# A two-layer graph-attention kernel: one attention block per turn, and a new order of the turn

## The chip, the cores and the metric

The kernel runs on one core of a Trainium2 chip. The metric is device time in microseconds (us) of one execution; a median of several runs is given, and one further execution was recorded by the hardware profiler. TensorE is called PE below, VectorE DVE, ScalarE ACT, GpSimd POOL, SyncE SP (its DMA queue SPq).

## What is computed

Input x is 128 graphs of 128 nodes with 512 features, adj a mask per graph. Two layers follow each other. Layer 0 is masked attention with 4 heads of 64, layer 1 layer-normalises its input once more, has 8 heads of 64 and lets each node see itself. All is float32.

```python
# layer 0
q, k, v = (split_heads(x @ W) for W in (Wq, Wk, Wv))
sim  = where(adj, q @ k.T * 64 ** -0.5, -max)
x    = layernorm(x + (softmax(sim) @ v) @ Wo + bo)
# layer 1
h    = layernorm(x) * gamma + beta
q, k, v = split(h @ w_qkv.T)
sim  = where(adj | eye, q @ k.T * 64 ** -0.5, -1e9)
out  = layernorm(x + (softmax(sim) @ v) @ w_out.T + b_out)
```

## The kernel before, in words

**Tiling.** Two graphs (b = 0, 1) make a group g; there are NG = 64 groups. R[g] holds a group's rows (128 nodes on the partitions, 2 x 512 features) from loading to storing. Every large matrix product (qkv of layer 0, qk and v of layer 1, and the output projections of both) is done as seven smaller block products in place of eight (1, 2, ..., 7 in the code, a Strassen-like scheme): sums of blocks of the activations are made by POOL (`sums`, `out_sums`, L281 to L291), sums of blocks of the weights once at the start by DVE (`weight_sums`). The products accumulate in three PSUM banks, "a", "f" and "c". `INTO` (L296) tells which product goes where, and which one starts its bank: 1, 6, 7, 4 go into a one after the other, 5 and 3 into f, 2 into c. After 1, 5 and 6 the running value is copied out by ACT (`eqk1`, `eqk5`, `eqk6` for layer 1's q and k, `ev` for v, `e` for layer 0), and the DVE later adds such a copy to what 2, 7 and 3 left. So product 7 cannot write bank a before ACT has read it for `eqk6`, and product 3 cannot write f before ACT has read it for `eqk5`.

**The pipeline over groups.** The kernel is an opening, a loop of turns `step(s)` for s = 2 to 63, and four turns `closing(s)`. All order is written out by hand (manual schedule): each engine carries its instructions out in the order in which the program issues them. A turn works on several groups at once: layer 0's qkv of group s (`product_0`), scores and softmax of layer 0 for group s - 1 and of layer 1 for group s - 3, attention and output projection of layer 0 for group s - 2 and of layer 1 for group s - 4, v and the last qk product of group s - 3, and qk of group s - 2.

**Attention before.** The turn has two half-turns, k = 2s and 2s + 1, one for each graph of a group. `scores(k)` (L435) computes the scores of both layers for one graph into four PSUM tiles; `cleared` (POOL) fills the softmax tiles with the mask value, `masked` (DVE, L466) copies the scores where the mask is set and takes the maxima, `exps` (ACT, L490) takes exponentials with their sums, `normalised` (L499, POOL) multiplies by the reciprocal sums. The transposition of the probabilities is done in three steps: `blocks` (L502) transposes 32 x 32 blocks on DVE, a DMA puts the result into DRAM (`put`, L204), and four DMAs fetch it with the blocks in place (`fetch`, L210, by `probs_arrive`). `attend(s)` (L543) multiplies the probabilities of both graphs and both layers by v, once per turn.

**Activations are transposed in the same way.** `turn(l, g)` (L219) transposes blocks of R[g] on DVE and puts them into DRAM (`scr`), `arrive` fetches four pieces (`raw`). For layer 0, `in_order(g)` (L246) copies raw to xT on ACT and calls `sums`; for layer 1, `finish(g, half)` (L259) does it with gamma and beta. `turn(0, s+1)` and `in_order(s+1)` bring the next group's xT for the next turn. In turns 2 and 3 (`direct`) layer 1's input is transposed on PE (`finish_direct`).

**Other steps.** `addend(l, g)` (L581, POOL) adds the bias to R[g]; for layer 1 ACT first scales R[g] by a ratio (L580). `out_product` (L421) adds each of its products to R[g] by a DVE addition (L425). `stats` (DVE) and `roots` (POOL) give mean and root; `norms` (ACT, L626, two rows) scales R[g], and is put on a list that `flush()` empties at its place in the order.

All DMAs are issued by SP, in program order. Near the turn's end the order before is:

```python
    p("qk", s - 2, 5, 6)
    in_order(s + 1)
    flush()
    p("qk", s - 2, 3, 7)
```

Of the kernel before, what the change touches and what calls it, by code (L numbers as in the profile page):

```python
# [27 lines left out]
def kernel(ctx: ExitStack, tc: tile.TileContext, x, adj, wq, wk, wv, wo, bo,  # L28
# [128 lines left out]
    def weight_sums(w, ws, *parts):  # L157
        for part in parts:
            for c in range(KH):
                if w is w1qk:  # L160
                    b11, b12 = w[:, c, :, 0], w[:, c, :, 1]
                    b21, b22 = w[:, KH + c, :, 0], w[:, KH + c, :, 1]
                else:
                    b11, b12 = w[:, c, 0], w[:, c, 1]
                    b21, b22 = w[:, KH + c, 0], w[:, KH + c, 1]
                part(b11, b12, b21, b22, ws[:, 0, c], ws[:, 1, c], ws[:, 2, c])

    def combine_1(b11, b12, b21, b22, t2, t3, t4):
        nc.vector.tensor_sub(b12, b12, b11)  # L169
        nc.vector.tensor_sub(t2, b22, b12)  # L170

    def combine_2(b11, b12, b21, b22, t2, t3, t4):
        nc.vector.tensor_sub(t3, t2, b11)
        nc.vector.tensor_sub(t4, b21, t2)

    def combine(*them):
        combine_1(*them)
        combine_2(*them)
# [35 lines left out]
    def turn(l, g):  # L214
        if not 0 <= g < NG:
            return
        t = one.tile([P, 4, G * KC * 32], F32, tag="turned_in", name=f"turned{l}_{g}")
        for b in range(G):
            nc.vector.transpose(t.rearrange("p a (b c i) -> p a b c i", b=G, c=KC)[:, :, b],  # L219
                                R[g][:, b].rearrange("p (c a i) -> p a c i", a=4, i=32))  # L220
        SCR[l] = put(t, f"scr{l}_{g}")
# [18 lines left out]
    def in_order(g):  # L240
# [7 lines left out]
        sums(0, g)  # L248
# [32 lines left out]
    def sums(l, g):  # L281
        xs = XS[l, g] = one.tile([P, 4, KH, N], F32, tag=f"xs{l}", name=f"xs{l}_{g}")
        halves_sums(xs, XT[l, g].rearrange("p (h c) (b n) -> p b h c n", h=2, b=2))
# [77 lines left out]
    def product_0(g, *which):  # L361
# [5 lines left out]
        for i in which:  # L367
# [23 lines left out]
            if i in (1, 5, 6):  # L391
                EV[0, i] = one.tile([P, 3 * P], F32, tag=f"e0_{i}", name=f"e0_{i}_{g}")
# [8 lines left out]
    def out_product(l, g, *which):  # L401
        if not 0 <= g < NG:
            return
        aT, so = AT[l, g], SO[l, g]
# [3 lines left out]
        for i in which:  # L408
            left = {1: aT[:, 0, :hk], 2: aT[:, 0, hk:], 3: so[:, 3], 4: aT[:, 1, hk:], 5: so[:, 0],
                    6: so[:, 1], 7: so[:, 2]}[i]  # L410
# [17 lines left out]
    SM, SUM, NMAX, PT, AT, SO = {}, {}, {}, {}, {}, {}  # L428

    def members(k):  # L430

        s, b = divmod(k, G)
        return [(l, g, b) for l, g in ((0, s - 1), (1, s - 3)) if 0 <= g < NG]

    def scores(k):  # L435
        both = members(k)
        made = []
        for l, g, b in both:
            H_ = HEADS[l]

            ps = [mm_tile(f"sc{l}_{g}_{b}_{s}").rearrange("p (k n) -> p k n", n=N) for s in range(2)]
            t = slice(b * N, (b + 1) * N)
            for h in range(H_):
                r = slice((h % 2) * D, (h % 2 + 1) * D)
                if l == 0:
                    q_, k_ = (QKV[g][r, b, h // 2, i, :] for i in range(2))
                else:
                    q_, k_ = (QK[1, g][r, i * H_ // 2 + h // 2, t] for i in range(2))
                nc.tensor.matmul(ps[h % 2][:, h // 2, :], q_, k_, start=True, stop=True)  # L449
            made.append((l, g, b, ps))  # L450
        return made
# [6 lines left out]
    def cleared(made, *layers):  # L458

        for l, g, b, ps in made:  # L460
            if l in layers:
                sm = SM[l, g, b] = two.tile([P, 2, HEADS[l] // 2, N], F32, tag=f"sm{l}", bufs=1,
                                            name=f"sm{l}_{g}_{b}")
                nc.gpsimd.memset(sm, (NEG0, NEG1)[l])  # L464

    def masked(made, layer):  # L466
        for l, g, b, ps in made:
            if l != layer:
                continue
            K = HEADS[l] // 2  # L470
            mask = M[g][:, b, :]
            sm = SM[l, g, b]
            for s in range(2):
                nc.vector.copy_predicated(sm[:, s], mask[:, None, :].to_broadcast([P, K, N]),  # L474
                                          ps[s][:, :K, :])
            nmax = three.tile([P, 2, K], F32, tag=f"nmax{l}", name=f"nmax{l}_{g}_{b}")
            nc.vector.tensor_reduce(nmax, sm, AX.X, ALU.max, negate=True)  # L477
            total = three.tile([P, 2, K], F32, tag=f"total{l}", name=f"total{l}_{g}_{b}")
            SUM[l, g, b], NMAX[l, g, b] = total, nmax

    def exps(l, k):
        b = k % G
        g = k // G - (1, 3)[l]
        if not 0 <= g < NG:
            return
        K = HEADS[l] // 2
        sm, nmax, total = SM[l, g, b], NMAX.pop((l, g, b)), SUM[l, g, b]
        for s in range(2):
            for k in range(K):
                nc.scalar.activation(sm[:, s, k, :], sm[:, s, k, :], AF.Exp, bias=nmax[:, s, k:k + 1],  # L490
                                     accum_out=total[:, s, k:k + 1])

    def normalised(k):
        for l, g, b in members(k):
            K = HEADS[l] // 2
            sm = SM[l, g, b]
            rec = three.tile([P, 2, K], F32, tag=f"rec{l}", name=f"rec{l}_{g}_{b}")
            nc.vector.reciprocal(rec, SUM.pop((l, g, b)))  # L498
            nc.gpsimd.tensor_tensor(sm, sm, rec[:, :, :, None].to_broadcast([P, 2, K, N]),  # L499
                                    op=ALU.mult)  # L500

    def blocks(k, *layers):  # L502


        both = members(k)
        if not both:
            return
        slots = {0: (0, HEADS[0]), 1: (HEADS[0], HEADS[0] + HEADS[1])}
        if 0 in layers:
            SCR["t"] = (one.tile([P, 4, sum(HEADS), 32], F32, tag="turned", name=f"turned_{k}"),  # L510
                        one.tile([P, 4, sum(HEADS), 32], F32, tag="pT", bufs=2, name=f"pT_{k}"))
        t, pT = SCR["t"]
        for l, g, b in both:
            if l in layers:
                lo, hi = slots[l]
                sm = SM.pop((l, g, b)).rearrange("p s k (q r) -> p q (s k) r", r=32)
                nc.vector.transpose(t[:, :, lo:hi, :], sm)  # L517
                PT[l, g, b] = pT[:, :, lo:hi, :]
        if 1 in layers:
            lo, hi = slots[both[0][0]][0], slots[both[-1][0]][1]  # L520
            t, pT = (u[:, :, lo:hi, :].rearrange("p a h i -> p a (h i)") for u in (t, pT))
            SCR["p", k] = pT, put(t, f"scrp{hi - lo}_{k}")

    def blocks_direct(k):

        for l, g, b in members(k):
            K = HEADS[l] // 2
            sm = SM.pop((l, g, b))
            pT = one.tile([P, 4, sum(HEADS), 32], F32, tag="pT", bufs=2, name=f"pT_{k}")
            PT[l, g, b] = pT[:, :, :2 * K, :]  # L530
            for s in range(2):
                pt = mm_tile(f"pt_{k}_{s}")
                for kk in range(K):
                    nc.tensor.transpose(pt[:, kk * N:(kk + 1) * N], sm[:, s, kk, :], ident)
                (nc.scalar.copy, nc.vector.tensor_copy)[s](
                    pT[:, :, s * K:(s + 1) * K, :].rearrange("p a h r -> p h a r"),
                    pt.rearrange("p (h a r) -> p h a r", h=K, a=4))

    def probs_arrive(k):
        if members(k):  # L540
            fetch(*SCR.pop(("p", k)))

    def attend(s):  # L543

        for l, g in ((0, s - 2), (1, s - 4)):
            if not 0 <= g < NG:
                continue
            K = HEADS[l] // 2
            aT = AT[l, g] = one.tile([P, G, K, N], F32, tag=f"aT{l}", name=f"aT{l}_{g}")
            for b in range(G):  # L550
                pT = PT.pop((l, g, b))
                if l == 1 or b == 0:
                    pm = mm_tile(f"av{l}_{g}_{b}").rearrange("p (k n) -> p k n", n=N)

                for h in range(HEADS[l]):
                    i, kk = h % 2, h // 2
                    o = pm[i * D:(i + 1) * D, (b * K if l == 0 else 0) + kk, :]
                    v = (QKV[g][:, b, kk, 2, i * D:(i + 1) * D] if l == 0
                         else V[1, g][:, b, h * D:(h + 1) * D])
                    nc.tensor.matmul(o.rearrange("p (a r) -> p a r", r=32), v, pT[:, :, i * K + kk, :],  # L560
                                     start=True, stop=True)
                if l == 1:
                    nc.scalar.copy(aT[:, b], pm)
                elif b == G - 1:
                    nc.scalar.copy(aT.rearrange("p b k n -> p (b k) n"), pm)  # L565
# [306 lines left out]
```

## Time and profile before

| what | value |
|---|---|
| median of 3 runs | 2863.34 us (2863.26 to 2864.84) |
| the profiled execution: its own time | 2865.48 us |
| its span, first to last instruction | 2863.7 us |
| mean granted TensorE clock | 0.996 of full speed |
| ACT busy, longest group (exps, L490) | 594.5 us, 1536 of 392 ns |
| POOL busy, longest group (bias, L581) | 303.0 us, 128 of 2367 ns |
| DMA traffic | 407.31 MB, mean 142 GB/s |
| start of turn 4 / of the first closing turn | 125.61 / 2740.37 us |

How to read it: the profile's page gives busy times of each engine, the chain of work that ended last, and groups of equal instructions. The timeline lists the instructions of an engine in order of time: start, length, engine, line, operation, output <- input, how many were merged, and in brackets the idle time before and what ended it. A float32 matmul stands as two rows in the counts. Matmuls overlap, so a price is best read from the distance between two starts. A DMA row's length is that of its issue; the time to landing is given apart.

### The profile page before, as it was taken

To read this page: it belongs to the slowest core of one execution; us is meant where nothing else is said; L and a number is where in the kernel's file an instruction comes from. 1 tells how busy PE (TensorE), PEld (TensorE's weight loads), DVE (VectorE), ACT (ScalarE), POOL (GpSimd) and SP (SyncE) were. 2 spreads that over 40 slices of the span, in tenths; PEclk is the share of its full clock that TensorE was granted. 3 is DMA by queue.
4 is the path that set the end of the run, shared out by engine and by line. 5 is a ranking of instruction groups with operands and counts; after the bars stand their busy time and mean duration, and the time that the engine had idled before them with its cause. 6 is when DMAs were issued, how large, how long until landed. Compare 5 with 4: busy or idle time off the path is not lost.

```text
span 2863.7 us, 62995 instructions
## 1 busy us (share of the span) xinstructions
PE 2818.6 (98%) x23297; PEld 2614.6 (91%) x23297; DVE 1824.1 (64%) x3625; ACT 1502.7 (52%) x4811; POOL 1758.7 (61%) x2439
## 2 busy tenths in 40 slices
PE   8899999999999999999999999999999999999997
PEld 7899999999999999999999999999999999999986
DVE  4666576666666666666666766666666666657664
ACT  3445555555555555555555555555555555555553
POOL 3566666666666666666666666666666666666654
PEclk9999999999999999999999999999999999999999
DMA  4354544544544545545545445445445455455432
GB/s 153 94 158 132 157 149 136 161 138 132 169 133 142 163 136 147 161 132 153 153 133 160 144 134 167 133 135 170 133 143 163 135 147 158 131 157 150 127 102 67
DMA packets 242707, 407.31 MB, mean 142 GB/s; under 512 B 40024, under 2 KB 175712, under 8 KB 242400
## 3 DMA queue, kind: packets, MB, share of 16 engines
q1 hardware_dynamic: 242400, 403.28, 47.8%
q8 instruction: 185, 3.03, 0.4%
q14 instruction: 122, 1.00, 0.1%
HBM read 206.05 MB, written 197.13 MB: 141 GB/s over the span
## 4 chain that ended last, share of the span: by engine, by line
PE 96%; DVE 2%; POOL 1%; ACT 1%; DMA 0%; issue 0%; SPq 0%; ACTq 0%; POOLq 0%; DVEq 0%
PE qka L328 16%; PE oa L421 12%; PE a L384 12%; PE va L328 8%; PE qkf L328 8%; PE sc L449 7%; PE f L384 6%; PE av L560 6%; PE of L421 6%; PE qkc L328 4%; PE vf L328 4%; PE c L384 3%; PE oc L421 3%; PE vc L328 2%; ACT sm L490 0%
## 5 line engine op out<-in xcount | busy, mean ns | idle before, releaser
L490 ACT ACTIVATE sm<-sm,nmax 128x128 f32<-128x128 f32 x1536 | 594.5, 392 | 265.6 <-DVE nmax L477 264.2
L499 POOL TENSOR_TENSOR sm<-sm,rec 128x512 f32<-128x512 f32 (+1 forms) x256 | 373.6, 1470 | 494.4 <-DVE rec L498 494.2
L474 DVE COPY_PREDICATED sm<-m,sc 128x512 f32<-128x512 uint8 (+1 forms) x512 | 269.0, 578 | 126.5 <-POOL sm L464 123.5
L291 POOL TENSOR_TENSOR xs<-xT 128x256 f32<-128x256 f32 x256 | 187.2, 731 | 253.8 <-ACT xT L246 192.9
L581 POOL TENSOR_TENSOR r<-r,bias 128x1024 f32<-128x1024 f32 x128 | 303.0, 2367 | 10.7 <-ACT r L580 10.7
L490 ACT ACTIVATION_READ_ACCUMULATOR sm<-sm,nmax 128x1 f32 x1536 | 293.2, 191 | 0.0
L517 DVE STREAM_TRANSPOSE turned<-sm 128x512 f32<-128x512 f32 (+1 forms) x255 | 239.8, 958 | 53.2 <-POOL sm L499 53.2
L328 PE MATMUL qka<-xs,wsqk 128*128 128x128 f32 x2048 | 249.7, 275 | 2.0 <-ACT eqk L354 2.0
L328 PE MATMUL qkf<-xs,w 128*128 128x128 f32 x2048 | 249.7, 275 | 0.9 <-DVE w L169 0.9
L477 DVE TENSOR_REDUCE nmax<-sm 128x4 f32<-128x512 f32 (+1 forms) x256 | 243.9, 953 | 8.8
L328 PEld LDWEIGHTS qkf<-xs,w 128*128 128x128 f32 x2048 | 243.6, 192 | 4.2 <-DVE w L169 1.1
L425 DVE TENSOR_TENSOR r<-oa,r 128x256 f32<-128x256 f32 x512 | 213.0, 416 | 49.8 <-PE oa L421 36.4
L354 ACT COPY ev<-va 128x256 f32<-128x256 f32 x128 | 47.6, 372 | 374.3 <-PE va L328 374.3
L328 PEld LDWEIGHTS qka<-xs,wsqk 128*128 128x128 f32 x2048 | 239.0, 192 | 2.1 <-issue 2.1
L291 POOL TENSOR_TENSOR so<-aT 128x128 f32<-128x128 f32 (+1 forms) x256 | 151.7, 593 | 126.3 <-ACT aT L565 111.7
L626 ACT ACTIVATE r<-r,shift,root 128x512 f32<-128x512 f32 x256 | 194.3, 806 | 46.8 <-POOL shift L615 46.7
L421 PE MATMUL oa<-wso,so 128*128 128x256 f32 x768 | 212.4, 385 | 4.9 <-DVE r L425 4.9
L421 PE MATMUL of<-wo,so 128*128 128x256 f32 x768 | 208.4, 380 | 1.2 <-POOL so L291 1.2
L359 DVE TENSOR_TENSOR qk<-qkf,eqk 128x512 f32<-128x512 f32 x64 | 44.2, 691 | 252.6 <-PE qkf L328 183.6
L354 ACT COPY eqk<-qka 128x512 f32<-128x512 f32 x128 | 75.1, 587 | 205.4 <-PE qka L328 205.4
L464 POOL MEMSET sm<- 128x512 f32 (+1 forms) x256 | 181.4, 738 | 2.1 <-DVE turned L517 2.1
L219 DVE STREAM_TRANSPOSE turned<-r 128x512 f32<-128x512 f32 x242 | 163.8, 697 | 26.3 <-ACT r L626 26.2
(140 smaller groups left out, 6598.0 us busy)
## 6 DMA issues: line engine op xcount, KB each, us to landing
scrp<-turned SPq DMA_DIRECT2D x124, 768.0 KB, 3.6
pT<-scrp SPq DMA_DIRECT2D x496, 192.0 KB, 4.3
scr<-turned SPq DMA_DIRECT2D x121, 512.0 KB, 2.6
raw<-scr SPq DMA_DIRECT2D x484, 128.0 KB, 3.2
r<-in_x_dram SPq DMA_DIRECT2D x64, 512.0 KB, 3.7
out_dram<-r SPq DMA_DIRECT2D x64, 512.0 KB, 2.8
m<-in_adj_dram SPq DMA_DIRECT2D x64, 32.0 KB, 3.8
raw_r<-in_L_gnn_w_qkv_dram SPq DMA_DIRECT2D x8, 256.0 KB, 4.3
```

The source lines that it names most:

```text
L291: nc.gpsimd.tensor_tensor(o, a0, a1, op=op)
L328: nc.tensor.matmul(o, lhsT, rhs, start=first and n == 0, stop=n == len(todo) - 1, skip_group_check=True)
L384: nc.tensor.matmul(acc[:, t * P:(t + 1) * P], lhsT, rhs, start=first and n == 0, stop=n == len(todo) - 1, skip_group_check=True)
L421: nc.tensor.matmul(acc, left[:, c], right[:, c], start=first and c == 0, stop=c == hk - 1, skip_group_check=True)
L425: nc.vector.tensor_add(part, acc, part)
L449: nc.tensor.matmul(ps[h % 2][:, h // 2, :], q_, k_, start=True, stop=True)
L474: nc.vector.copy_predicated(sm[:, s], mask[:, None, :].to_broadcast([P, K, N]), ps[s][:, :K, :])
L477: nc.vector.tensor_reduce(nmax, sm, AX.X, ALU.max, negate=True)
L490: nc.scalar.activation(sm[:, s, k, :], sm[:, s, k, :], AF.Exp, bias=nmax[:, s, k:k + 1], accum_out=total[:, s, k:k + 1])
L499: nc.gpsimd.tensor_tensor(sm, sm, rec[:, :, :, None].to_broadcast([P, 2, K, N]), op=ALU.mult)
L517: nc.vector.transpose(t[:, :, lo:hi, :], sm)
L581: nc.gpsimd.tensor_tensor(R[g], R[g], (bias0, bias1)[l][:, None, :].to_broadcast([P, G, E]), op=ALU.add)
```

## The change

**What it does.** There are no half-turns any more. `scores(s)` computes, in one block at the start of the turn, three parts: part 0 is layer 0 with both graphs (2 x 4 heads), parts 1 and 2 are layer 1 with one graph each (8 heads). Each part has tiles of the same size, 128 x 1024. Part 1 uses the PSUM banks a0 and f0. `attend(s)` follows directly. All steps of the softmax go by parts, and each part has its own put and its own four fetches; before, a half-turn's put carried both layers. All other steps of the turn have a new order; qk product 4 moves from the next turn to the end of its own turn. `in_order` no longer calls `sums`; `sums(0, s+1)` stands between qk 3 and 4. The DVE's block transposes share one tag with two buffers. The opening transposes the first probabilities on PE (`blocks_direct`). The last four turns become `closing(NG)`, `closing(NG + 1)` and `last()`; in `last`, the output projection of the last group is done without the seven-product scheme (`out_plain`, 4 matmuls of 512 columns for each graph, with one root and one store for each graph).

The counts of the large products and of score and attention matmuls of a turn are unchanged. The order on ACT in the second half of a turn, in the changed kernel: copies of v, finish (4), eqk1, in_order (2), eqk6, ratio (2), norms (2), eqk5, the copy of qk 4. The order of the DMAs on SP in a turn: two loads; puts of scrp0, scr1, scrp1; fetch of raw1 (4), of pT0 (4); puts of scrp2, scr0; fetches of pT1 (4), pT2 (4), raw0 (4); the store.

**The diff, cut to its core.**

```diff
     def turn(l, g):
-        t = one.tile([P, 4, G * KC * 32], F32, tag="turned_in", name=f"turned{l}_{g}")
+        t = one.tile([P, 4, G * KC * 32], F32, tag="turned", bufs=2, name=f"turned{l}_{g}")
...
     def in_order(g):
...
-        sums(0, g)
...
-    def scores(k):
-        both = members(k)
-        made = []
-        for l, g, b in both:
-            ps = [mm_tile(f"sc{l}_{g}_{b}_{s}").rearrange("p (k n) -> p k n", n=N) for s in range(2)]
...
+    def scores(s):
+        made = {}
+        for part in PARTS:
+            g = group_of(s, part)
+            if part == 1:
+                ps = [ps_st.tile([P, 512], F32, tag=t, name=f"sc{part}_{g}_{t}") for t in ("a0", "f0")]
+            else:
+                ps = [mm_tile(f"sc{part}_{g}_{i}") for i in range(2)]
...
+    def blocks(s, *parts):
+        for part in parts:
+            if group_of(s, part) is not None:
+                t = one.tile([P, 4, 2 * K1 * 32], F32, tag="turned", bufs=2, name=f"turnedp{part}_{s}")
+                nc.vector.transpose(t.rearrange("p q (h r) -> p q h r", r=32),
+                                    SM.pop(part).rearrange("p i k (q r) -> p q (i k) r", r=32))
+                SCR["p", part] = put(t, f"scrp{part}_{s}")
+
+    def probs_arrive(s, *parts):
+        for part in parts:
+            if group_of(s, part) is not None:
+                fetch(turned_tile(s, part).rearrange("p a h i -> p a (h i)"), SCR.pop(("p", part)))
...
     def step(s):
-        k = 2 * s
         direct = s in (2, 3)
+        made = scores(s)
         load(s + 1)
-        made = scores(k)
-        cleared(made, 0, 1)
-        masked(made, 0)
-        masked(made, 1)
...
+        masked(made, s, 0, 1, 2)
+        attend(s)
+        maxima(s, 0, 1)
+        out_sums(0, s - 2)
+        exps(s, 0, 0)
         product_0(s, 1)
+        exps(s, 0, 1)
         out_product(0, s - 2, 1, 5, 2)
+        maxima(s, 2)
+        product_0(s, 2)
+        normalised(s, 0)
+        out_product(0, s - 2, 6, 3)
+        exps(s, 1, 0)
+        stats(0, s - 2, 0)
+        product_0(s, 6)
+        exps(s, 1, 1)
+        out_product(0, s - 2, 7)
+        product_0(s, 5)
         out_product(0, s - 2, 4)
         stats(0, s - 2, 1)
+        exps(s, 2, 0)
         product_0(s, 7)
+        exps(s, 2, 1)
+        normalised(s, 1)
+        product_0(s, 3)
+        blocks(s, 0)
         flush()
+        product_0(s, 4)
...
+            turn(1, s - 2)
+        out_sums(1, s - 4)
+        v(s - 3, 1, 2)
+        out_product(1, s - 4, 1)
+        blocks(s, 1)
+            arrive(1, s - 2)
+        probs_arrive(s, 0)
+        v(s - 3, 6, 5)
+        out_product(1, s - 4, 2)
+        normalised(s, 2)
+        v(s - 3, 7, 3, 4)
+        flush(latest)
+        cleared(s + 1, 0, 1)
...
             finish(s - 2, 0)
+        blocks(s, 2)
+        cleared(s + 1, 2)
+        out_product(1, s - 4, 6, 5)
+        turn(0, s + 1)
         if not direct:
             finish(s - 2, 1)
-            turn(0, s + 1)
...
+        out_product(1, s - 4, 7, 3)
+        probs_arrive(s, 1, 2)
+        arrive(0, s + 1)
         stats(1, s - 4, 0)
-        p("qk", s - 2, 1, 2)
+        qk(s - 2, 1)
+        addend(0, s - 1)
         out_product(1, s - 4, 4)
         stats(1, s - 4, 1)
-        p("qk", s - 2, 5, 6)
+        with_self(s - 2)
+        qk(s - 2, 2)
         in_order(s + 1)
+        qk(s - 2, 6)
+        addend(1, s - 3)
         flush()
-        p("qk", s - 2, 3, 7)
+        qk(s - 2, 5, 7, 3)
+        sums(0, s + 1)
+        qk(s - 2, 4)
...
-    for s in range(NG, NG + 4):
-        closing(s)
+    closing(NG)
+    closing(NG + 1)
+    last()
```

## The prediction, made before the changed kernel was run

> **What bounds the kernel now.** I read the page's busy shares and its chain that ended last, then the timeline of one turn of the loop (999.87 us, where a turn's first score matmul starts, to 1043.38 us), engine by engine.
>
> ```profile
> PE 2818.6 (98%) x23297; PEld 2614.6 (91%) x23297; DVE 1824.1 (64%) x3625; ACT 1502.7 (52%) x4811; POOL 1758.7 (61%) x2439
> PE 96%; DVE 2%; POOL 1%; ACT 1%; DMA 0%; issue 0%; SPq 0%; ACTq 0%; POOLq 0%; DVEq 0%
> ```
>
> TensorE (PE) is busy for 98% of the span and holds 96% of the chain: a turn is as long as PE's instructions plus whatever PE waits. So I ask two things: do PE's own instructions get shorter, and does PE wait anew. First PE itself (columns: start us, length, engine, line, operation):
>
> ```profile
> 999.87 0.71 PE L449 MATMUL sc<-qkv 64*128 64x128 f32 x8
> 1000.42 1.06 PE L449 MATMUL sc<-qk 64*128 64x128 f32 x16
> 1001.41 2.05 PE L328 MATMUL qka<-xT,wsqk 128*128 128x128 f32 x16
> 1003.30 1.06 PE L384 MATMUL a<-xT,w 128*128 128x128 f32 x8
> 1004.19 0.61 PE L384 MATMUL a<-w,xT 128*128 128x128 f32 x4
> 1004.73 1.09 PE L560 MATMUL av<-pT,qkv 128*64 128x128 f32 x16
> 1005.66 1.92 PE L560 MATMUL av<-pT,v 128*64 128x128 f32 x32
> 1007.50 1.16 PE L384 MATMUL f<-xs,w 128*128 128x128 f32 x8
> 1008.50 0.61 PE L384 MATMUL f<-w,xs 128*128 128x128 f32 x4
> ...
> 1039.72 1.95 PE L328 MATMUL qkf<-xs,w 128*128 128x128 f32 x16
> 1041.51 1.95 PE L328 MATMUL qka<-xs,wsqk 128*128 128x128 f32 x16
> 1043.38 0.38 PE L449 MATMUL sc<-qkv 64*128 64x128 f32 x2
> ```
>
> The reader takes prices from differences of starts. A qk product is 1.79 (1039.72 to 1041.51), a layer-0 product 1.34, an output product 0.43 (layer 0) or 0.86 (layer 1), a v product 0.86. Entering or leaving the scores or the attention products adds about 0.1: 1041.51 to 1043.38 is 1.87, qka after the scores 1.89. Eight score rows take 0.55, sixteen 0.99, not twice as much. Next the end of that turn on DVE, on SyncE's queue (SPq) and on ACT, one fence each:
>
> ```profile
> 1031.39 1.29 DVE L219 STREAM_TRANSPOSE turned<-r 128x512 f32<-128x512 f32 x2
> ```
>
> ```profile
> 1032.71 0.34 SPq L204 DMA_DIRECT2D scr<-turned  x1
> 1034.76 0.34 SPq L204 DMA_DIRECT2D scrp<-turned  x1
> 1035.49 2.56 SPq L210 DMA_DIRECT2D raw<-scr  x4
> 1038.45 1.73 SPq L210 DMA_DIRECT2D pT<-scrp  x4
> ```
>
> ```profile
> 1038.18 0.59 ACT L354 COPY eqk<-qkf 128x512 f32<-128x512 f32 x1 [3.84 <-PE qkf L328]
> 1039.97 0.59 ACT L354 COPY eqk<-qka 128x512 f32<-128x512 f32 x1 [1.21 <-PE qka L328]
> 1041.38 1.14 ACT L246 COPY xT<-raw 128x512 f32<-128x512 f32 x2 [0.82 <-DMA raw<-scr]
> 1042.43 1.51 ACT L626 ACTIVATE r<-r,shift,root 128x512 f32<-128x512 f32 x2
> ```
>
> This is the transposed input of the next group: turned by DVE (turn, done 1032.68), put to DRAM, fetched in four pieces, copied by ACT (in_order) at 1041.38, where ACT had waited 0.82 for the data. The trip takes 8.7 us; in five other turns of the trace 8.34, 8.38, 8.43, 8.74 and 9.19. It harms nothing before, because both eqk copies that PE needs stand ahead of it on ACT.
>
> **What the Trainium skill says.** "Perfetto Trace Analysis", Sequencer Loop: a sequencer reads the next instruction and the instruction waits for its semaphores; so what is queued behind waits too. The ACT rows agree: norms (L626) begins only after in_order. The same page, DMA Instruction — HWDGE: the reported time of a DMA ends with its issue, the data movement lies outside; here a piece issues in 0.44 us (1.76 for 4) and lands about 3.4 us after. "DMA: Bandwidth & Descriptors", Anatomy of one DMA, gives about 2.0 us plus bytes/436 GB/s per DMA, fitted on GpSimd's path: my estimate from it is 3.2 us for the 512 KB put and 2.3 for a 128 KB piece, with 1.3 of issue between 6.8 us. The trace's 8.3 to 9.2 decides.
>
> **The change, part by part.** I count t in us from a turn's first score matmul.
>
> *PE's own work.* The matmuls of a turn are the same. Scores become three groups of sixteen rows, 3 x 0.99 = 2.97 (before 2 x 1.54 = 3.08), attention 2.77 as before, directly behind. Leaving and entering happen once, 0.2, instead of twice for the scores and once for attention; whether scores to attention costs another 0.1 the trace does not show (bounds 0 and 0.2, I take 0.1). Walked without waits: attention ends at 5.85; seven layer-0 and seven layer-0 output products (9.38 + 3.01) end at 18.2; v and layer-1 output fill to 26.0; output product 6 to 26.9, 5 to 27.7, 7 and 3 to 29.5; qk 1 to 31.3, output 4 to 32.1, qk 2 and 6 to 35.7, qk 5 to 37.5, qk 7 to 39.3, qk 3 and 4 to 42.8, with entry 42.9. Before: 2610 between the start of turn 4 (125.6) and, 60 turns later, 2740.4 is 43.58 a turn. That is 0.65 less a turn.
>
> *DVE, POOL, softmax.* Six masks of 0.67 (4.0) replace eight (4.2); ends of the softmax chain: masks to 5.3, maxima to 7.6, 24 exps of 0.385 on ACT with the evacuations to 17.9, norms to 19.4. Nothing on PE waits for it inside the turn: probabilities are used a turn later. Hidden by 25 us of PE; costs nothing. One small wait: the part-2 transpose waits for POOL's normalisation (to 26.2), DVE gets to the add of output product 6 at 27.5, and product 7 on the same bank waits about 0.2. If the wait below stands, this is absorbed by it.
>
> *turn and in_order, the deciding step.* turn(0,s+1) now stands on DVE behind the add of output product 5: 27.7 + 0.2 + 0.35, then 1.29, plus some 0.2 of DVE backlog: done at t = 29.8 (before 32.8). But on SP eight fetches (pT1, pT2) now stand between its put and its own four: 8 x 0.44 = 3.5, so the first piece goes at +3.9 instead of +2.8 (1032.68 to 1035.49); in return no larger pT fetch follows close behind. The trip is bounded by 8.3 (the shortest before: the extra queue absorbed) and 10.2 (longest before, 9.2, plus 1.1). I take 9.0: last piece at +5.5, landing 3.4. So in_order starts at 38.8. And it stands on ACT ahead of the copy of qk product 6 (eqk6), ratio, norms and the copy of qk 5 (eqk5). Who waits: PE's qk 7 writes the bank that eqk6 reads, and qk 3 the bank that eqk5 reads.
> - in_order 38.8, two copies 1.05 (1041.38 to 1042.43): eqk6 starts 39.85, ends 40.44, PE about 0.1 later: qk 7 starts at 40.5 instead of 37.5. **Wait 3.0.**
> - behind eqk6: 0.46 to the next start, ratio 1.23 (two rows at 1012.65), norms 1.43: eqk5 starts 42.97, ends 43.56: qk 3 starts at 43.66 instead of 42.29. **Wait 1.4.**
> - qk 3 and 4 with entry 3.66: the turn ends at 47.3.
> 47.3 less 43.58 is 3.7 a turn; turns 4 to 63 are 60: **+224 us**.
>
> *finish.* raw1 is turned at 20.3, its trip before was 7.7 to 8.5, so finish starts at 28.0 to 28.8 and qk 1 (29.5) waits at most 0.4; absorbed as well.
>
> *Opening and ends.* The opening loses a DRAM round trip (about -5). Turns 2 and 3 meet the same in_order wait with little PE work behind the turn, about 6 each (+12). Before, the last four turns take 2740.4 to 2863.7, 123 us. After: two turns without layer-0 products (42.9 - 9.4 + 2.1 of transposes + 1 of waits, about 36.5 each) and the last (26.5 of PE, 7 of tail, about 34): 107, so -16. Sum -9.
>
> Sum on the profiled execution's time, 2865.5 (span 2863.7): 2865.5 + 224 - 9 = 3080. The median of the runs is 2.1 lower: **3078**.
>
> **The rivals.**
> - *The data come in time* (the other side: faster). Without a DRAM trip worth speaking of, eqk6 starts at 35.9, eqk5 ends at 39.65, qk 3 waits 0.5, the turn is 43.4: 60 x -0.18 = -11, with -9 for the ends 2843. It decides where in_order starts at 35.2 or earlier, a trip of 5.4 us. For it: less DRAM traffic of 768 KB in one piece. Against: every trip of these six takes 8.3 or more, and SP has more to issue. Chance 0.08.
> - *The trip is stretched further*: each piece waits for one eight DMAs ahead of it to land (the fetch of raw took 2.56 instead of 1.76), and waits ahead of turn (output 7, qk 1, DVE's buffers) move its start. With a trip of 11 and turn at 30.3 the turn is 49.8: +373, 3227. Chance 0.12.
> - *The stall is covered and the switches saved whole*: 42.9 a turn, 2865.5 - 39 - 9 - 2 = 2815. It needs in_order before 34.9 and ratio and norms out of eqk5's way; its chance, 0.01, I count as faster.
> - No effect, waits and savings equal: 0.02.
>
> **How the numbers follow.** My case has 0.77: with trips of 8.3 to 10.2 and turn at 29.6 to 30.1 the turn is 46.4 to 48.8, 3018 to 3170 with the ends. The range 3010 to 3165 covers most of it and touches the longer rival. Within 0.2% (6 us) a measurement can't tell from no change. Faster 0.09, same 0.02, slower 0.89.
>
> **What would show it.** Right: turns of about 47 us; PE's wait list led by qka and qkf waiting for ACT's eqk, some 3 and 1.4 us each turn; ACT idle for DMA raw<-scr ahead of in_order at t near 38; scores and attention about 5.8 together. Wrong: PE still 98% busy, or the long wait in another place (attention waiting for pT, the layer-0 products for a bank of scores), or in_order starting before t = 35.

## The result and the profile after

| kernel | median us | ratio to before, 95% interval |
|---|---|---|
| before | 2863.69 | |
| changed | 3283.91 (3275.7 to 3285.39) | 1.1461 [1.1441, 1.1481] |

The kernel became 14.6% slower; the profiled execution's span is 3283.4 us, its mean granted TensorE clock 0.94 (before 0.996). The prediction had the direction, the place and the first cause, and half of the size: 3078 us, range 3010 to 3165.

Starts of turns on PE divide the difference of the two spans, 419.7 us: turn 4 starts at 130.78 instead of 125.61 (+5.2), the 60 turns from there take 50.62 each instead of 43.58 (+422.6), and the end from the first closing turn takes 115.2 instead of 123.3 (-8.1).

From the page of the changed kernel, the busy line and two of the costliest groups (after the bar: busy us in all, mean ns of one; last part: idle time ahead of it on its engine, and what ended it):

```profile
PE 2967.3 (90%) x23301; PEld 2764.5 (84%) x23301; DVE 1815.3 (55%) x3301; ACT 1503.3 (46%) x4813; POOL 1760.3 (54%) x2311
L322 PE MATMUL qka<-xs,wsqk 128*128 128x128 f32 x2048 | 355.7, 346 | 282.3 <-ACT eqk L348 282.3
L239 ACT COPY xT<-raw 128x512 f32<-128x512 f32 x122 | 69.3, 615 | 514.4 <-DMA raw<-scr 514.4
```

The first group in the kernel before:

```profile
L328 PE MATMUL qka<-xs,wsqk 128*128 128x128 f32 x2048 | 249.7, 275 | 2.0 <-ACT eqk L354 2.0
```

PE is down to 90%, and one group has the wait: qk products that follow eqk, 282.3 us over the run (before 2.0), and in_order on ACT waited 514.4 us for raw. Before, the rows of the same form took 275 ns; here 346 ns on average. That is the part which the prediction did not have. The end of one turn (it runs from 1042.94 to 1093.57) on PE:

```profile
1078.89 1.95 PE L322 MATMUL qkf<-xs,w 128*128 128x128 f32 x16
1085.50 3.75 PE L322 MATMUL qka<-xs,wsqk 128*128 128x128 f32 x16 [4.67 <-ACT eqk L348]
1089.05 2.81 PE L322 MATMUL qkf<-xs,w 128*128 128x128 f32 x16
1091.69 1.95 PE L322 MATMUL qka<-xT,wsqk 128*128 128x128 f32 x16
```

qk 5 starts at 1078.89 and is through 1.79 later. qk 7 starts 4.8 after that, and it takes 3.55 (1085.50 to 1089.05) in place of 1.79; qk 3 takes 2.64; qk 4 is at 1.88 again. The same stretch on DVE, SP and ACT:

```profile
1071.13 1.29 DVE L212 STREAM_TRANSPOSE turned<-r 128x512 f32<-128x512 f32 x2
```

```profile
1072.46 0.34 SPq L197 DMA_DIRECT2D scr<-turned  x1
1072.89 4.19 SPq L203 DMA_DIRECT2D pT<-scrp  x8
1077.31 2.50 SPq L203 DMA_DIRECT2D raw<-scr  x4
```

```profile
1083.74 1.14 ACT L239 COPY xT<-raw 128x512 f32<-128x512 f32 x2 [8.50 <-DMA raw<-scr]
1084.78 0.58 ACT L348 COPY eqk<-qka 128x512 f32<-128x512 f32 x1
1085.26 1.33 ACT L588 ACTIVATE r<-r,ratio 128x512 f32<-128x512 f32 x2
1086.49 1.50 ACT L634 ACTIVATE r<-r,shift,root 128x512 f32<-128x512 f32 x2
1087.90 0.56 ACT L348 COPY eqk<-qkf 128x512 f32<-128x512 f32 x1
```

turn is done at 1072.42; the fetch of raw begins 4.9 later, behind the eight others; ACT idles 8.50 us for it, copies, and only then comes eqk6, for which qk 7 has waited. The trip (from the end of turn to the start of in_order) is 11.3 us here, and 10.7 to 12.2, mean 11.5, over the 59 turns that have one; before it was 8.3 to 10.1, mean 8.7. The stretches of those products in a table (us; busy time and count of PE, PEld, DVE, ACT, POOL; granted clock; DMA share; GB/s):

```profile
1042.90:1078.90 36.00, 35.97 (x300) 33.44 (x300) 26.40 (x49) 18.64 (x67) 20.48 (x27) 1.00 0.46 138
1085.50:1089.05 3.55, 3.55 (x17) 3.55 (x17) 0.00 (x0) 2.97 (x5) 2.38 (x2) 0.50 0.02 6
1089.05:1091.69 2.64, 2.64 (x18) 2.64 (x17) 0.69 (x1) 0.00 (x0) 2.48 (x4) 0.66 0.51 191
```

The granted clock is 0.50 in qk 7 and 0.66 in qk 3, after 1.00 in the turn up to the wait. The 0.66 is a mean: the trace's record of the clock has 0.50 from 1084.00, still in the wait, to 1090.83, in the middle of qk 3, and 1.00 after it. Half clock comes in each of the 59 turns that have an in_order. DMA is nearly still (0.02) in the slowest stretch, so traffic is not what slows it there.

The trace holds a first experiment by itself: turn 63 has no next group, so no turn(0) and no in_order. It takes 44.0 us, where the 59 others take 49.1 to 51.5.

### The profile page after: what moved, and what is told of

It reads as the page before. It is cut to its first block, busy times and chain, and to the rows that moved or that the text cites. A ratio compares the mean times of both kernels' runs of the same rounds, so it can differ in the third digit from the quotient of the medians.

```text
span 3283.4 us, 63013 instructions
## 1 busy us (share of the span) xinstructions
PE 2967.3 (90%) x23301; PEld 2764.5 (84%) x23301; DVE 1815.3 (55%) x3301; ACT 1503.3 (46%) x4813; POOL 1760.3 (54%) x2311
## 4 chain that ended last, share of the span: by engine, by line
PE 53%; DMA 24%; SPq 6%; DVE 6%; issue 4%; ACT 2%; POOL 1%; ACTq 0%; DVEq 0%; POOLq 0%
DMA raw<-scr 12%; PE qka L322 10%; PE a L378 8%; DMA pT<-scrp 8%; SPq L203 6%; PE av L568 5%; PE qkf L322 5%; PE f L378 5%; PE oa L416 4%; DMA scrp<-turnedp 4%; DVE turnedp L522 4%; PE c L378 2%; PE of L416 2%; PE sc L449 2%; PE va L322 2%
## 5 line engine op out<-in xcount | busy, mean ns | idle before, releaser
L322 PE MATMUL qka<-xs,wsqk 128*128 128x128 f32 x2048 | 355.7, 346 | 282.3 <-ACT eqk L348 282.3
L322 PEld LDWEIGHTS qka<-xs,wsqk 128*128 128x128 f32 x2048 | 334.7, 256 | 292.1 <-issue 292.1
L507 POOL TENSOR_TENSOR sm<-sm,rec 128x1024 f32<-128x1024 f32 x192 | 364.4, 1898 | 388.9 <-DVE rec L506 388.5
L239 ACT COPY xT<-raw 128x512 f32<-128x512 f32 x122 | 69.3, 615 | 514.4 <-DMA raw<-scr 514.4
L322 PEld LDWEIGHTS qkf<-xs,w 128*128 128x128 f32 x2048 | 294.7, 229 | 1.4 <-ACT eqk L348 1.4
L522 DVE STREAM_TRANSPOSE turnedp<-sm 128x1024 f32<-128x1024 f32 x189 | 234.7, 1242 | 45.7 <-POOL sm L507 32.8
L483 DVE COPY_PREDICATED sm<-m,sc 128x512 f32<-128x512 uint8 x256 | 172.1, 725 | 135.2 <-PE sc L449 112.5
L489 DVE TENSOR_REDUCE nmax<-sm 128x8 f32<-128x1024 f32 x192 | 226.2, 1204 | 0.1
L251 ACT ACTIVATE xT<-raw,gb 128x256 f32<-128x256 f32 x240 | 124.7, 590 | 147.8 <-DMA raw<-scr 147.8
L600 DVE BATCH_NORM_STATS2 st<-r 128x6 f32<-128x512 f32 x254 | 176.5, 695 | 8.7
```

What stands on the lines that cost most here:

```text
L322: nc.tensor.matmul(o, lhsT, rhs, start=first and n == 0, stop=n == len(todo) - 1, skip_group_check=True)
L489: nc.vector.tensor_reduce(NMAX[part], SM[part], AX.X, ALU.max, negate=True)
L507: nc.gpsimd.tensor_tensor(SM[part], SM[part], rec[:, :, :, None].to_broadcast([P, 2, K1, N]), op=ALU.mult)
L522: nc.vector.transpose(t.rearrange("p q (h r) -> p q h r", r=32), SM.pop(part).rearrange("p i k (q r) -> p q (i k) r", r=32))
```

## The experiments

All times are medians, with the ratio to the kernel before on the same chip and its 95% interval. "A turn" is the mean of turns 4 to 63 unless it says otherwise. The diffs of e1 to e4 are against the changed kernel, that of e5 against the kernel before, those of e6 and e9 against e2.

**e1: in_order alone back behind eqk5**, in step(s):

```diff
         qk(s - 2, 2)
-        in_order(s + 1)
         qk(s - 2, 6)
         addend(1, s - 3)
         flush()
-        qk(s - 2, 5, 7, 3)
+        qk(s - 2, 5)
+        in_order(s + 1)
+        qk(s - 2, 7, 3)
```

> The changed kernel, with in_order alone moved on ACT from ahead of eqk6 to behind eqk5. Theory (PE waits because eqk6 stands behind in_order on ACT, and the wait also slows the next two qk products): the wait of 4.8 us ahead of qk 7 and the slow products (2.6 us more) are gone; left is a wait of about 0.5 us ahead of qk 3 for eqk5, which still stands behind ratio and norms; turns of 43.7 us, 2862 us. Rival (the longer trip through DRAM is the bound, wherever in_order stands): the wait moves to the first layer-0 product of the next turn, turns stay above 48 us, over 3100 us.

Measured: 2877.25 us, 1.0045 [1.003, 1.006], granted clock 0.998. One call's place is thus worth 407 us. The trip is as long as before the move (mean 11.4 us), so it is the place on ACT, not the trip by itself, that PE felt. The wait that was left is there, at qk 3, with its cause in the row ahead of it:

```profile
1034.11 1.95 PE L322 MATMUL qka<-xs,wsqk 128*128 128x128 f32 x16
1036.32 2.05 PE L322 MATMUL qkf<-xs,w 128*128 128x128 f32 x16 [0.26 <-ACT eqk L348]
```

qk 3 starts 2.21 after qk 7 in place of 1.79. The shortest turns are 43.63 (expected 43.7); the mean is 44.1, as longer ones wait up to 0.52 at qk 3 and at times at qk 1 for finish.

**e2: ratio and norms behind eqk5 too** (eqk6, eqk5, ratio, norms, in_order on ACT):

```diff
-        in_order(s + 1)
         qk(s - 2, 6)
+        qk(s - 2, 5)
         addend(1, s - 3)
         flush()
-        qk(s - 2, 5, 7, 3)
+        in_order(s + 1)
+        qk(s - 2, 7, 3)
```

> As the first, and ratio and norms are behind eqk5 too. Theory: nothing on PE waits at the end of the turn, turns of 43.2 us, 2824 us, below the kernel before (2863.7) by what the single attention block saves. Rival (the block's own order costs more than it saves): 2863 us or more, with waits in the scores or the attention products.

Measured: 2835.66 us, 0.9904 [0.9887, 0.992]: below the kernel before. The shortest turns are 43.11, the mean 43.40. Of the 31.1 us that the span (2832.6) is shorter than before, 12.9 come from the opening with turns 2 and 3 (turn 4 starts at 112.75), 11 from the turns, 7 from the end. The new turn gives 0.2 of the expected 0.65 us here: the shortest turns lie 0.2 above the predicted 42.9, and the mean holds another 0.3, most of it waits at qk 1 for finish (up to 1.2 us in a turn).

**e3: PE kept busy while it waits**, in turns 4 to 63 of the changed kernel; the matmuls' result is used by nothing:

```diff
-        qk(s - 2, 5, 7, 3)
+        qk(s - 2, 5)
+        if s >= 4:
+            extra = mm_tile(f"extra_{s}")
+            for n in range(19):
+                nc.tensor.matmul(extra[:, :P], ident, ident, start=True, stop=True)
+        qk(s - 2, 7, 3)
```

> The changed kernel, with 19 matmuls of the identity with itself (4.2 us of PE, their result unused) between qk 5 and qk 7 of turns 4 to 63, where PE waits. Theory (the slow products 7 and 3 come from PE's idleness ahead of them): qk 7 takes 1.8 us again instead of 3.55, qk 3 waits 1.2 us for eqk5 and then takes 1.8, turns of 49.2 us instead of 50.6, about 3200 us, mean granted clock back near 1.0. Rival (they are slow for another reason, such as the DMA traffic at that moment): qk 7 stays at 3.5 us, the time stays at 3284 us.

Measured: 3215.99 us, 1.1229 [1.1212, 1.1246], clock 0.997; it falls in none of turns 4 to 63. More work on PE made the kernel 68 us faster:

```profile
1006.98 4.41 PE L802 MATMUL extra<-ident 128*128 128x128 f32 x38
1011.87 2.02 PE L322 MATMUL qka<-xs,wsqk 128*128 128x128 f32 x16 [0.49 <-ACT eqk L348]
1014.89 2.05 PE L322 MATMUL qkf<-xs,w 128*128 128x128 f32 x16 [1.00 <-ACT eqk L348]
1016.78 1.95 PE L322 MATMUL qka<-xT,wsqk 128*128 128x128 f32 x16
```

qk 7 has a length of 2.02 in place of 3.75, and qk 3 is through in 1.89 (1014.89 to 1016.78). So the products were slow because PE had idled. Now the wait for eqk5 behind ratio and norms appears, 1.0 idle: in the changed kernel the slow qk 7 had covered it. A turn is 49.5, expected 49.2.

**e8: fifteen such matmuls in place of nineteen**, so that PE idles longer:

> As e3_pe_kept_busy with 15 matmuls in place of 19: PE idles about 1.4 us ahead of qk 7 (0.5 there, 2.1 to 2.4 in e4_fetch_first, 4.7 in the changed kernel). If the products slow down only after waits of more than 1.4 us: the time of e3_pe_kept_busy, 3216 us. If they slow down already after this: qk 7 of 3 us or more, 3250 us or more.

Measured: 3224.01 us, 1.1248 [1.1231, 1.1265], against 1.1229 with nineteen.

```profile
1014.59 2.02 PE L322 MATMUL qka<-xs,wsqk 128*128 128x128 f32 x16 [1.24 <-ACT eqk L348]
```

PE idles 1.4 us on average ahead of qk 7 and up to 2.2; the clock falls in one of the 59 turns, after a wait of 2.01. The start of qk 3, 3.02 after qk 7 as with nineteen, would not show it by itself: qk 3 waits for eqk5 (1.0 idle) and so would hide a somewhat slower qk 7. Here it is the record of the clock, and the length of qk 7 (2.02), that tell that it ran at full rate.

**e4: the fetch of raw ahead of the eight others:**

```diff
-        probs_arrive(s, 1, 2)
         arrive(0, s + 1)
+        probs_arrive(s, 1, 2)
```

> The changed kernel, with the fetch of raw0 ahead of the eight fetches of probabilities on SP. Theory (the trip grew from 8.6 to 11.3 us because of the eight fetches issued ahead): in_order starts 8.4 to 9.2 us after the turn's transposition, at 38.2 instead of 40.8 us of the turn; qk 7 waits 2.2 us; turns of 46.7 us if the clock stays up after that wait, 47.7 if it drops as now: 3050 to 3110 us. Rival (the trip is long because DRAM and the engines are loaded with as much data as before, whatever the order): in_order at 40 us or later, 3250 us or more.

Measured: 3081.55 us, 1.0755 [1.0727, 1.0783]. in_order starts 9.0 us after turn in the turn shown (1009.57 to 1018.55), 9.1 on average, so the eight fetches ahead cost 2.4 us of the trip. PE waits 0.9 to 3.3 us ahead of qk 7, mean 2.2, and the clock falls in 31 of the 59 turns. One turn of each kind, and the longer wait is the one without the fall:

```profile
1020.32 3.29 PE L322 MATMUL qka<-xs,wsqk 128*128 128x128 f32 x16 [2.14 <-ACT eqk L348]
1496.27 2.02 PE L322 MATMUL qka<-xs,wsqk 128*128 128x128 f32 x16 [2.84 <-ACT eqk L348]
```

The first qk 7 has a length of 3.29 at a granted clock of 0.58, the second 2.02 at 1.00. A turn is 47.4, between the two variants of the expectation (46.7 with the clock up, 47.7 with the drop), as both kinds of turn occur.

**e7: ratio and norms alone behind eqk5**, in_order left ahead of eqk6 (in the changed kernel's step, qk 5 moves ahead of addend and flush):

> The changed kernel, with ratio and norms alone moved behind eqk5; in_order stays ahead of eqk6. Theory (the slow qk 7 of 3.5 us already covers the 3.1 us in which eqk5 stood behind ratio and norms): no change, 3275 to 3290 us. Rival (ratio and norms cost their 1.4 us on top): 3200 us.

Measured: 3282.02 us, 1.1452 [1.1433, 1.1472]: no difference from 3283.91. The 1.4 us that the prediction charged for this wait was covered.

**e5: in_order ahead in the kernel before:**

```diff
-    p("qk", s - 2, 5, 6)
     in_order(s + 1)
+    p("qk", s - 2, 5, 6)
     flush()
```

> The kernel before, with in_order alone moved ahead of qk 5 and 6, and so on ACT ahead of eqk5 and eqk6. Theory (this one place makes the loss, with the old half-turns too): qk 3 waits for eqk5 behind in_order, from 1039.7 to 1043.1 of the turn shown, 3.4 us, and the next two products are slow by 2.4 us: turns of 49.4 us, about 3215 us. Rival (the loss belongs to the new block with its eight fetches ahead): within 1% of 2864 us.

Measured: 3193.38 us, 1.1147 [1.113, 1.1164]. A turn is 48.9 and shows the same pair, a wait and a product at low clock:

```profile
1006.04 3.38 PE L328 MATMUL qkf<-xs,w 128*128 128x128 f32 x16 [3.40 <-ACT eqk L354]
1009.21 2.27 PE L328 MATMUL qka<-xs,wsqk 128*128 128x128 f32 x16
```

The old half-turns lose 328 us from this one place; the rival that the new block is needed for it falls.

**e6: taking the remaining waits off e2:** the part-2 transposition behind DVE's adds of output products 6 and 5, and product 4 ahead of qk 1:

```diff
-        blocks(s, 2)
-        cleared(s + 1, 2)
         out_product(1, s - 4, 6, 5)
+        blocks(s, 2)
+        cleared(s + 1, 2)
...
-        qk(s - 2, 1)
-        addend(0, s - 1)
         out_product(1, s - 4, 4)
         stats(1, s - 4, 1)
+        qk(s - 2, 1)
+        addend(0, s - 1)
```

> As e2_all_behind, with the part-2 transposition behind DVE's adds of output products 6 and 5, and output product 4 ahead of qk 1. Theory (turns of 43.41 us there hold 0.26 us of waits at output products 7 and 3 and 0.3 us at qk 1 for finish): both go, turns of 42.9 us, about 2805 us. Rival (the distance to 42.9 us lies in the switches between kinds of matmuls): 2830 to 2836 us.

Measured: 2904.55 us, 1.0137 [1.0122, 1.0152]: a miss, slower than before. Both small waits are gone, but a new one of 1.44 stands in nearly every turn (44.54 us):

```profile
1035.76 1.03 PE L416 MATMUL of<-wo,so 128*128 128x256 f32 x4
1038.23 1.13 PE L416 MATMUL oa<-wso,aT 128*128 128x256 f32 x4 [1.44 <-DVE r L420]
```

```profile
1035.44 1.24 DVE L522 STREAM_TRANSPOSE turnedp<-sm 128x1024 f32<-128x1024 f32 x1
1036.60 1.26 DVE L212 STREAM_TRANSPOSE turned<-r 128x512 f32<-128x512 f32 x2
1037.79 0.39 DVE L420 TENSOR_TENSOR r<-oa,r 128x256 f32<-128x256 f32 x1
```

Output product 4 writes the bank that the add of product 7 reads, and that add (1037.79) stood on DVE behind two transpositions of 2.4 us together. The same mistake as in_order's, on another engine.

**e9: turn behind the adds of output products 7 and 3 instead** (blocks left where e2 has it, the fetch of raw first, product 4 ahead of qk 1):

```diff
-        turn(0, s + 1)
...
         out_product(1, s - 4, 7, 3)
-        probs_arrive(s, 1, 2)
+        turn(0, s + 1)
         arrive(0, s + 1)
+        probs_arrive(s, 1, 2)
         stats(1, s - 4, 0)
-        qk(s - 2, 1)
-        addend(0, s - 1)
         out_product(1, s - 4, 4)
         stats(1, s - 4, 1)
+        qk(s - 2, 1)
+        addend(0, s - 1)
```

> As e2_all_behind, with turn behind DVE's adds of output products 7 and 3, the fetch of raw0 ahead of those of the probabilities, and output product 4 ahead of qk 1. In e6_waits_off the wait of 0.3 us at qk 1 went, but product 4 waited 1.44 us for an add that stood behind a transposition and turn on DVE. Theory (a wait at the end of an add's queue, not the order on PE, took the gain): here product 4 finds its add done, qk 1 finds finish done, and turn comes 2 us later with 9 us of trip to in_order, just in time behind norms: turns of 43.1 us, about 2816 us. Rival (the turn moved later makes in_order late for the next turn, or the waits only change places): 2835 us or more.

Measured: 2819.33 us, 0.9841 [0.9827, 0.9854], the fastest of all. Nearly all turns are 43.10 to 43.12 (mean 43.15). The wait at qk 1 for finish is gone; in e2 that one had varied from turn to turn (turns of 43.1 to 45.0) with the landing of raw. e9 moves three things at once, and what each of them gives was not separated.

## Why the prediction was right or wrong

**PE's own work: right.** Scores and attention take 5.65 us together in the turn shown (predicted 5.85): attention 2.77 as predicted, the scores 2.88 where the prediction had 2.97, and the 0.1 for the switch between them does not show. The turn without waits was put at 42.9; the floor that the runs show is 43.11, and the difference is the wait at output product 7, which the prediction had (0.2; 1070.59 would have been the start, 1070.78 it was in the changed kernel).

**The deciding step, in_order ahead of eqk6: right in place and chain.** e1 and e5 show it both ways: taken out of the changed kernel it returns 407 us, put into the kernel before it costs 328 us. The rival "the data come in time" falls: the trip is 11.3 us, its deciding point was 5.4.

**The trip was mis-sized: 9.0 predicted, upper bound 10.2, measured 11.3** (mean of all turns 11.5, none under 10.6). The failed term is the queue ahead: I let the first fetch go at +3.9 us and the last at +5.5, they go at +4.9 and about +7.0; and I let landing take 3.4 where it is 4.4 from the last issue (1079.38) to 1083.74. e4 shows that the eight fetches ahead make 2.4 us of trip. Together with turn being done 0.3 earlier, qk 7 starts at t = 42.56 and not 40.5: +2.1 us a turn. The rival "the trip is stretched further", to which I gave 0.12, had this size of trip (11), a time of 3227, and the reason: SP holds a fetch back until the one eight ahead of it has landed. The trace shows it: the first fetch of raw goes at 1077.31, and the fetch eight ahead of it landed at 1077.24. No DMA there goes before the landing of the one eight ahead, where the trace tells it, and 159 fetches of raw go within 0.12 us of it; in the kernel before none does. Only the rival's other reason, a later turn, did not come (done at 29.5, not 30.3).

**The step that failed altogether: that the products after the wait keep their old price (1.79 us), put in without a reason.** After the wait qk 7 takes 3.55 and qk 3 2.64, 2.6 us more. In their shade the 1.4 us wait for eqk5 vanished (e7: no difference; e3: it comes back as 1.0 idle when the clock stays up). From the start of qk 7 to the turn's end I had 6.8 us, the trace has 8.07: +1.3. So 2.1 + 1.3 = 3.4 a turn against 3.3 missed (50.62 less 47.3).

This was to be seen before: in the kernel before PE waited 4.42 us once, in turn 3, and the sixteen attention rows after it took 1.91 us from start to start (88.91 to 90.82, granted clock 0.50) where the turn shown has 0.93:

```profile
88.91 1.98 PE L560 MATMUL av<-pT,qkv 128*64 128x128 f32 x16 [4.42 <-DVE sm L474]
```

The Trainium skill states it as well: "TensorE: Matmul & The Clock Gate", What's actually happening: PE's clock is halved after an idle window of about 3.4 us and back after about as long a busy one. The traces agree on half speed (0.50) and on the length: each of the 64 low stretches in the changed kernel's trace lasts 3.4 us or about two or three times that, 6.8 in most. They differ on the wait that is enough, see below.

**Opening and ends: right in sign.** Turn 4 came 5.2 later (predicted +7), but two errors cancel there: turn 2 starts 10.6 earlier (38.41 instead of 48.98, predicted 5), and turns 2 and 3 take 15.7 more (predicted 12). The end gave 8.1 (predicted 16): the last part has waits of 1.78, 1.18, 1.54 and 2.66 us that I had put at 1 us a turn.

## What to carry to other kernels

An instruction that waits for a DMA holds everything behind it on its engine (here eqk6, while ACT idled 8.50 us). Before it is moved up, list what stands behind it, and which of that the bounding engine waits for; a copy out of PSUM that frees a bank belongs ahead of it. Price a new wait on PE not only by its length: in turns 4 to 63 of these runs each wait of 3 us or more, and some from 1.8 us up, put PE's next work at half clock; and look whether the slow work hides another wait. Look also for the copies and adds on other engines that PE waits for: e6 lost 1.44 us a turn at the add of one output product, which in e9 found its engine free.

## What the runs showed of the hardware

- The clock goes by a grid. In these traces the granted clock is 1.00 or 0.50, and it falls only at points of a grid of 3.41 us that runs through the whole execution (the 64 falls in the changed kernel's trace and the 35 in e4's lie on theirs within 0.01 us).
- So the length of a wait alone does not decide. In turns 4 to 63 of all these traces no wait of PE under 1.8 us was followed by half clock, every one of 3.0 us or more was, and in between both happened: in e4 a wait of 1.89 was enough in one turn and one of 2.90 was not in another. What separates them is how much of the wait falls into one interval of the grid. My estimate from the traces: half clock follows an interval in which PE idles for more than about 1.8 to 2.0 us (none with less than 1.77, all with more than 1.97), and full clock follows again after one in which it idles for less than about 0.6.
- The same section of the skill says that the window of about 3.4 us runs freely; the grid agrees with that. It speaks of a whole idle window; here a good half of one was enough.
- Filling a wait with useless matmuls can be worth it: 4.2 us of them a turn made the kernel 2% faster (3283.91 to 3215.99).
